# Another timetable in a fused attention and state-space kernel: projection two steps ahead, ScalarE's table blocks and GpSimd's products in chosen slots

## The chip, the cores and the metric

The kernel runs on one core of a Trainium2 chip. The metric is the device time of one launch in microseconds (us). A core has five engines with one instruction stream each, executed in order: TensorE (PE in the profile; its weight loads are PEld), VectorE (DVE), ScalarE (ACT), GpSimd (POOL) and SyncE (SP), which in this kernel issues nearly all DMA transfers. An engine waits at an instruction until the semaphores that this instruction names have been raised by others, and everything behind it in its stream waits too.

## The reference, cut to what matters

The input is a map of 2 x 256 x 256 positions with 128 channels, in float32. Layer 0 is a row-wise attention; it is not touched by the change. Layer 1 is a selective state-space layer over the 65,536 positions of each image, read as one sequence:

```python
xz = x @ in_proj_w.T                       # x: 128 channels, group-normalised; xz: 2 * 256
xi, z = jnp.split(xz, 2, axis=-1)
xi = silu(depthwise_conv_3x3(xi) + conv_b) # 256 channels
xs = xi.reshape(B, D_INNER, L)             # D_INNER = 256, L = 65536
x_dbl = jnp.einsum('bdl,cd->bcl', xs, x_proj_w[0])
dts, Bs, Cs = x_dbl[:, :8], x_dbl[:, 8:24], x_dbl[:, 24:]
delta = softplus(jnp.einsum('brl,dr->bdl', dts, dt_w[0]) + dt_b[0][None, :, None])
A = -jnp.exp(A_logs)                       # 256 x 16
# for each channel d and state n, along the sequence:
#   h = exp(delta * A) * h + (delta * xs) * B ;  y = sum over n of h * C
y = selective_scan(xs, delta, A, Bs, Cs, Ds)   # adds Ds * xs
y = layernorm(y) * ln_g + ln_b
y = y * silu(z)
return y @ out_proj_w.T                    # and the layer's input is added
```

## The kernel before, in words

First come statistics of layer 0, its attention and the statistics of layer 1; this stage ends at about 3,340 us and is the same in both kernels. The rest is the state-space layer. Each image is cut into 64 steps of four image rows, T = 1024 positions, so there are 128 steps. The 256 channels times 16 states of a step are computed in 32 **units** (NU = 32): a unit holds 32 channels times 4 states on the 128 partitions, and 1024 positions along the free dimension. A unit is named by h (half of the channels), m (four states) and q (32 channels).

The order of the work is written out by hand: a loop over **slots** t emits for each engine what belongs to slot t, and the streams of TensorE, VectorE, ScalarE and GpSimd keep that order. SP's stream is not fixed by hand; the framework orders it. In slot t stand, in this order: the loads for unit t+6 (`fetch`), GpSimd's product for unit t+2 (`drive`, hb = du * B), GpSimd's product of unit t-1 if that unit is "pooled" (`product`, yc = h * C), ScalarE's exponential of unit t+1 (`decay`, da = exp(delta * A), into one of two PSUM buffers), VectorE's `scan` of unit t and, if the unit is not pooled, its `product` on VectorE too, every fourth slot TensorE's sum over states (`add_up`), every sixteenth the copy of the sum to SBUF (`y_out`), then the pieces that were entered for this slot with `at(slot, piece)`, and last ScalarE's copy of the scan's last column (`remember`). A scan of a pooled unit writes over hb in SBUF, that of another over da in PSUM. Ten of 32 units are pooled: before, those with t * 10 % 32 < 10, that is 0, 4, 7, 10, 13, 16, 20, 23, 26, 29.

The pieces come from two functions. `project(k)` makes the inputs of step k's scans: `load` (raw rows), `begin`, `turn` and `normalise` (transposed and group-normalised xn), `keep` (two halo rows for the next step), `conv` (nine products on TensorE for each of four 512-wide groups; the three with one row offset dy are one piece), `conv_out`, `silu_xs`, `gate` and `gate_out` (z, one product for each group, and its copy into the tile sz), `silu_z`, `states` and `states_out` (delta's low-rank input, B and C), `size` and `size_out` (the argument of softplus, into the tile delta), `softplus`, and `times` (du = delta * xs, on GpSimd). xs, sz, B and C, delta and du are stored to DRAM and loaded again, spread over partitions, by `fetch` and by `finish`. `conv`, `gate`, `states`, `size` and `turn` share one PSUM buffer (tag "p"). The tiles xs, sz, delta and du have one buffer each. `finish(k)` normalises the rows of y, multiplies by silu(z), projects and writes the result; its ScalarE pieces stand in slots 6, 14, 22, 30 (`norm`), 0, 8, 16, 24 (`affine`) and 3, 11, 19, 27 (`leave`) of the step after, its row statistics on VectorE in slots 4, 12, 20, 28, its product with silu(z) on VectorE (`gated`) in slots 1, 9, 17, 25, and `scales` on GpSimd in 5, 13, 21, 29. `finish` is not changed.

Before, project(k) has base = 32 k - 36, so conv begins in slot 30 of step k-2 and the last piece stands in slot 25 of step k-1. silu_xs is in slot 14, the two softplus in 19 and 22, silu_z in 25. Exponential, silu and softplus need different tables in ScalarE, so each of these four blocks has a table load ahead of it and one ahead of the decay that follows.

Of the kernel before, what the change touches and what calls it, by code (L numbers as in the profile page):

```python
# [8 lines left out]
F32 = mybir.dt.float32  # L9
AF = mybir.ActivationFunctionType  # L10
ALU = mybir.AluOpType
# [4 lines left out]
P = 128  # L16
# [5 lines left out]
def attn_then_ssm_kernel(  # L22
# [26 lines left out]
    nc = tc.nc  # L49
# [5 lines left out]
    NH = DI // P  # L55
    NS = A_logs.shape[1]
    DR = dt_w.shape[2]
    TB = 512
# [72 lines left out]
    with tc.tile_pool(name="prep", bufs=1) as prep, tc.tile_pool(  # L131
        name="prep2", bufs=3
# [14 lines left out]
        for g in range(NCG):  # L147
            for m in range(NSG):
                nc.sync.dma_start(
                    out=alog_d[:, :, g, m],  # L150
                    in_=A_logs[g * CQ : (g + 1) * CQ, m * SR : (m + 1) * SR],
# [70 lines left out]
    with tc.tile_pool(name="st", bufs=2) as stp, tc.tile_pool(  # L222
        name="st_x", bufs=3
    ) as stx, tc.tile_pool(name="st_ps", bufs=2, space=PSUM) as st_ps:
        for b in range(B):
            stats = stp.tile([P, G, NT, 6], F32, name="stats")
            for k in range(NT):
                xt = stx.tile([P, TT, C], F32, name="xt")
                nc.sync.dma_start(
                    out=xt,  # L230
                    in_=x_tok[b, k * P * TT : (k + 1) * P * TT, :].rearrange(
                        "(p t) c -> p t c", p=P
                    ),
# [15 lines left out]
    with ExitStack() as actx:  # L249
# [117 lines left out]
        for b in range(B):  # L367
# [17 lines left out]
            for g in range(NG):  # L385
# [4 lines left out]
                for gr in range(G):  # L390
                    nc.vector.bn_stats(stats1[:, gr, g, :], x1g[:, :, :, gr * CG : (gr + 1) * CG])
                nc.gpsimd.dma_start(  # L392
                    out=x1[b][:, g * LG : (g + 1) * LG, :].rearrange("(i p) l c -> p i l c", p=P),
                    in_=x1g,
# [8 lines left out]
    T = R * W  # L403
    NSTEP = H // R
    NB = T // TB
    WP = W + 2
    RB = TB // W
    WT = W // P
    NU = NCG * NSG
    NM = NQ * NSG  # L410
    POOLED = 10
    s1 = ctx.enter_context(tc.tile_pool(name="s1", bufs=1))
    s2 = ctx.enter_context(tc.tile_pool(name="s2", bufs=2))
    s3 = ctx.enter_context(tc.tile_pool(name="s3", bufs=3))
# [6 lines left out]
    dr = ctx.enter_context(tc.tile_pool(name="dr", bufs=3, space=DRAM))  # L421
# [6 lines left out]
    def at(t, piece, *args):  # L428
        slots.setdefault(t, []).append((piece, args))
# [4 lines left out]
    def project(k):  # L434

        b, s = steps[k]
        rs, sh = gn1[b]
        base = k * NU - NU - 4
        n = min(R, H - 1 - R * s)
        v = given[k] = {}  # L440
        o = {}
# [127 lines left out]
            )  # L569

        def size_out(h, i):
            if i == 0:
                o["delta"] = s1.tile([P, T], F32, name="delta")
            nc.scalar.activation(
                o["delta"][:, i * TB : (i + 1) * TB],
                o["dt"],
                AF.Identity,
                bias=dtb_c[:, h : h + 1],
            )

        def softplus(h):
            nc.scalar.activation(o["delta"], o["delta"], AF.Softplus)
            if h == 0:
                v["delta"] = dr.tile([NH, P, T], F32, name="delta_d")
                v["du"] = dr.tile([NH, P, T], F32, name="du_d")
            nc.sync.dma_start(out=v["delta"][h], in_=o["delta"])

        def times(h):
            du = s1.tile([P, T], F32, name="du")
            nc.gpsimd.tensor_tensor(du, o["delta"], o["xs"][:, h, :], ALU.mult)  # L590
            nc.sync.dma_start(out=v["du"][h], in_=du)

        at(base - 12, load)
        at(base - 3, begin)
        for r in range(0, n, RB):
            at(base - 3 + r, turn, "raw", r, min(RB, n - r))
            at(base - 2 + r, normalise, 2 + r, min(RB, n - r))
        at(base - 1 + RB, keep)
        t = base + 2
        for h in range(NH):  # L600
            for i in range(NB):
                for dy in range(3):
                    at(t + dy, conv, h, i, dy)
                at(t + 3, conv_out, h, i)
                t += 4

        at(t, silu_xs)
        at(t, gate, 0, 0)
        at(t + 1, gate_out, 0, 0)
        at(t + 1, states, 0)  # L610
        at(t + 2, states_out, 0)
        at(t + 2, states, 1)
        at(t + 3, states_out, 1)
        at(t + 3, size, 0, 0)
        at(t + 4, size_out, 0, 0)
        at(t + 4, size, 0, 1)
        at(t + 5, size_out, 0, 1)
        at(t + 5, softplus, 0)
        at(t + 5, gate, 0, 1)
        at(t + 6, gate_out, 0, 1)  # L620
        at(t + 6, times, 0)
        at(t + 6, size, 1, 0)
        at(t + 7, size_out, 1, 0)
        at(t + 7, size, 1, 1)
        at(t + 8, size_out, 1, 1)
        at(t + 8, softplus, 1)
        at(t + 8, gate, 1, 0)
        at(t + 9, gate_out, 1, 0)
        at(t + 9, times, 1)
        at(t + 9, gate, 1, 1)  # L630
        at(t + 10, gate_out, 1, 1)
        at(t + 11, silu_z)

    def finish(k):

# [138 lines left out]
                )  # L774

    def pooled(t):
        return t % NU * POOLED % NU < POOLED

    def decay(t):
        k, h, m, q = unit(t)  # L780
# [12 lines left out]
    def scan(t):  # L793
        k, h, m, q = unit(t)
        u = units[t]
        st = states_of[steps[k][0]][:, h * NQ + q, m : m + 1]
        u["h"] = u["hb"] if pooled(t) else u["da"]
        nc.vector.tensor_tensor_scan(u["h"], u["da"], u["hb"], st, ALU.mult, ALU.add)  # L798
# [6 lines left out]
    def product(t):  # L805
        k, h, m, q = unit(t)
        u = units[t]
        u["yc"] = s8.tile([P, T], F32, name="yc")
        eng = nc.gpsimd if pooled(t) else nc.vector
        eng.tensor_tensor(u["yc"], u["h"], repeats["cc", k, h, m], ALU.mult)  # L810
# [34 lines left out]
    for k in range(len(steps)):  # L845
        project(k)
        finish(k)
# [8 lines left out]
    with tc.manual_schedule(engines=engines):  # L856
        for t in range(min(slots), max(slots) + 1):
            if 0 <= t + AHEAD < end:
                fetch(t + AHEAD)
            if 0 <= t < end and t % (NU * NSTEP) == 0:  # L860
                st = s1.tile([P, NCG, NSG], F32, name="state")
                nc.gpsimd.memset(st, 0.0)
                states_of[steps[t // NU][0]] = st
            if 0 <= t + 2 < end:
                drive(t + 2)
            if 0 <= t - 1 < end and pooled(t - 1):
                product(t - 1)
            if 0 <= t + 1 < end:
                decay(t + 1)
            if 0 <= t < end:  # L870
                scan(t)
                if not pooled(t):
                    product(t)
            if 0 <= t - 5 < end and (t - 5) % NQ == 0:
                add_up(t - 5)
            if 0 <= t - 6 < end and unit(t - 6)[2:] == (NSG - 1, 0):
                y_out(t - 6)
            for piece, args in slots.pop(t, ()):
                piece(*args)
            if 0 <= t < end:  # L880
                remember(t)
# [37 lines left out]
```

## Time and profile before

| what | value |
|---|---|
| median of 3 runs | 18,758.38 us (18,757.69 to 18,761.69) |
| the profiled execution | 18,753.55 us, its span 18,751.8 us |
| VectorE busy over the span | 15,569.1 us (83%) |
| GpSimd busy | 13,905.4 us (74%) |
| TensorE busy | 14,378.9 us (77%) |
| ScalarE busy | 11,203.5 us (60%) |
| DMA, mean over the span | 184 GB/s, SP's queue 52.6% of 16 engines |

The profile is of one execution. A group line names the source line, engine and operation, the tiles written and read, how many instructions it holds, then their busy time and the mean in ns of one, then the idle time of the engine just ahead of them and the engine and line that ended most of it. A timeline line begins with the start in us from the span's start and the time busy; a bracket at its end holds the idle time ahead and what ended it. Times of single instructions overlap a little, so sums of them can be some per cent above the time that passed. In the stretch from 3,500 to 18,700 us VectorE is busy 13,525.82 of 15,200 us and GpSimd 13,795.43.

### The profile page before, as it was taken

Reading aid. Unit: us, or ns where it says so; the run is one execution under the profiler, and the core shown is the slowest. Engines: PE = TensorE matmul, PEld = TensorE weight load, DVE = VectorE, ACT = ScalarE, POOL = GpSimd, SP = SyncE. Lnnn points to the kernel's source line nnn. Section 1 sums busy time; section 2 is a strip of 40 time slices with the busy share of each in tenths; the row PEclk is TensorE's granted clock in tenths of the full one; section 3 lists DMA queues with packets and bytes.
Section 4 is the critical chain, followed back from the end, with each engine's and each line's share of the span. In section 5 each row is a group of like instructions: output and inputs, shape, how many; then the busy total and the mean of one; then the engine's idle time right before and its main releaser. Section 6 shows DMA issues by size and latency. Waiting matters only on the chain. (4 is left out here: it accounts for less than half of the span.)

```text
span 18751.8 us, 175838 instructions
## 1 busy us (share of the span) xinstructions
PE 14378.9 (77%) x54327; PEld 6530.2 (35%) x54327; DVE 15569.1 (83%) x14782; ACT 11203.5 (60%) x18207; POOL 13905.4 (74%) x8236
## 2 busy tenths in 40 slices
PE   4999999777777777777777777777777777777776
PEld 3666666222222222222222222222222222222222
DVE  6555555688888888888888888888888888888888
ACT  2444444566666666666666666666666666666665
POOL 0000000699999999999999999999999999999998
PEclk7999999888888888888888888888888888888887
DMA  4111111566666666666666666666666656666664
GB/s 190 68 68 54 68 68 59 172 208 207 208 210 207 208 209 209 208 209 206 206 209 209 207 208 208 208 208 208 210 207 208 207 206 209 210 207 209 207 209 169
DMA packets 1428682, 3451.87 MB, mean 184 GB/s; under 512 B 121836, under 2 KB 712984, under 8 KB 1409304
## 3 DMA queue, kind: packets, MB, share of 16 engines
q1 hardware_dynamic: 1419032, 3373.50, 52.6%
q0 software_dynamic: 8704, 67.11, 0.8%
q8 instruction: 428, 7.01, 0.2%
q14 instruction: 518, 4.24, 0.1%
HBM read 2752.28 MB, written 687.88 MB: 183 GB/s over the span
## 5 line engine op out<-in xcount | busy, mean ns | idle before, releaser
L791 POOL TENSOR_TENSOR hb<-du_r,bb 128x1024 f32<-128x1024 f32 x4096 | 9556.8, 2357 | 0.2 <-issue 0.2
L798 DVE TENSOR_TENSOR_SCAN da<-da,state,hb 128x1024 f32<-128x1024 f32 x2816 | 6608.6, 2347 | 1360.3 <-ACT da L783 1203.4
L783 ACT ACTIVATE da<-delta_r,a_neg 128x1024 f32<-128x1024 f32 x4096 | 4574.6, 1117 | 484.5 <-DVE hb L798 408.3
L497 PE MATMUL u_ps<-xn,w_tap 128*128 128x512 f32 x9216 | 4444.8, 630 | 24.6 <-ACT xs L508 6.1
L810 DVE TENSOR_TENSOR yc<-da,cc 128x1024 f32<-128x1024 f32 x2816 | 3449.5, 1225 | 160.4 <-issue 1.8
L798 DVE TENSOR_TENSOR_SCAN hb<-da,state,hb 128x1024 f32<-128x1024 f32 x1280 | 2995.4, 2340 | 208.4 <-ACT da L783 122.0
L810 POOL TENSOR_TENSOR yc<-hb,cc 128x1024 f32<-128x1024 f32 x1280 | 3014.5, 2355 | 6.0 <-issue 4.6
L830 PE MATMUL y<-yc,sel 128*32 128x512 f32 x16384 | 2564.9, 665 | 146.9 <-POOL yc L810 141.2
L497 PEld LDWEIGHTS u_ps<-xn,w_tap 128*128 128x128 f32 x9216 | 1802.0, 205 | 2158.4 <-issue 1911.7
L803 ACT COPY state<-da 128x1 f32<-128x1 f32 x2816 | 437.0, 155 | 3142.3 <-DVE yc L810 3142.3
L392 POOL DMA_DIRECT2D x<-x1g x32 | 23.2, 726 | 3033.6 <-DVE x1g L360 3033.6
L545 PE MATMUL xd_ps<-xs,w_xp 128*64 128x512 f32 x1024 | 935.3, 1068 | 793.8 <-ACT state L803 705.7
L590 POOL TENSOR_TENSOR du<-delta,xs 128x1024 f32<-128x1024 f32 x256 | 599.1, 2340 | 899.2 <-ACT state L803 761.3
L830 PEld LDWEIGHTS y<-yc,sel 128*32 128x32 f32 x16384 | 525.7, 116 | 2047.9 <-issue 1270.0
L563 PE MATMUL dt_ps<-xd,w_dt 8*128 8x512 f32 x1024 | 696.1, 765 | 541.6 <-ACT sz L533 538.6
L522 PE MATMUL z_ps<-xn,w_z 128*128 128x512 f32 x1024 | 582.8, 651 | 612.7 <-ACT sz L533 483.4
L695 PE MATMUL yd<-ident,yn 128*128 128x128 f32 x2048 | 373.0, 312 | 813.8 <-ACT yn L683 813.8
L717 PE MATMUL o_ps<-xres,ident 128*128 128x256 f32 x1024 | 413.0, 491 | 520.6 <-DVE yg L713 520.5
L657 PE MATMUL yt<-ident,ys 128*128 128x128 f32 x2048 | 331.3, 285 | 529.7 <-ACT ob L730 529.7
L823 PE MATMUL y<-xr,d_diag 128*128 128x512 f32 x1024 | 722.4, 845 | 0.0
L720 PEld LDWEIGHTS o_ps<-w_out,yg 128*128 128x128 f32 x4096 | 671.0, 233 | 45.1
L312 ACT ACTIVATE e<-s_ps,nmx 128x256 f32<-128x256 f32 x1024 | 471.7, 472 | 355.4 <-DVE nmx L308 354.9
(134 smaller groups left out, 18302.7 us busy)
## 6 DMA issues: line engine op xcount, KB each, us to landing
bb<-bc_d SPq DMA_DIRECT2D x1024, 512.0 KB, 4.2
cc<-bc_d SPq DMA_DIRECT2D x1024, 512.0 KB, 4.9
delta_r<-delta_d SPq DMA_DIRECT2D x1024, 512.0 KB, 6.4
du_r<-du_d SPq DMA_DIRECT2D x1024, 512.0 KB, 4.8
xs_d<-xs SPq DMA_DIRECT2D x128, 1024.0 KB, 7.8
xr<-xs_d SPq DMA_DIRECT2D x256, 512.0 KB, 4.4
delta_d<-delta SPq DMA_DIRECT2D x256, 512.0 KB, 2.6
du_d<-du SPq DMA_DIRECT2D x256, 512.0 KB, 2.6
```

Source lines behind the costliest of these rows:

```text
L497: nc.tensor.matmul(o["u"], w_tap[:, h, 3 * dy + dx, :], o["xn"][:, i * RB + dy : i * RB + dy + RB, dx : dx + W], start=(dy == 0 and dx == ...
L522: nc.tensor.matmul(o["z"], w_z[:, h, :], o["xn"][:, 1 + i * RB : 1 + (i + 1) * RB, 1 : W + 1], start=True, stop=True,)
L545: nc.tensor.matmul(o["xd_ps"], w_xp[:, h, :], o["xs"][:, h, i * TB : (i + 1) * TB], start=(h == 0), stop=(h == NH - 1),)
L563: nc.tensor.matmul(o["dt"], w_dt[:, h, :], o["xd"][0:DR, i * TB : (i + 1) * TB], start=True, stop=True,)
L590: nc.gpsimd.tensor_tensor(du, o["delta"], o["xs"][:, h, :], ALU.mult)
L720: nc.tensor.matmul(o["o"][:, j, :], o["yg"][:, h, j * P : (j + 1) * P], w_out[:, h, :], start=False, stop=(j == WT - 1 and h == NH - 1),)
L783: nc.scalar.activation(da, spreads["delta", k, h, q], AF.Exp, scale=a_neg[:, g, m : m + 1])
L791: nc.gpsimd.tensor_tensor(hb, spreads["du", k, h, q], repeats["bb", k, h, m], ALU.mult)
L798: nc.vector.tensor_tensor_scan(u["h"], u["da"], u["hb"], st, ALU.mult, ALU.add)
L810: eng.tensor_tensor(u["yc"], u["h"], repeats["cc", k, h, m], ALU.mult)
L823: nc.tensor.matmul(y[:, cols], d_diag[:, h, :], xr[:, cols], start=True, stop=False)
L830: nc.tensor.matmul(y[q * CQ : (q + 1) * CQ, cols], sel, units[t + q]["yc"][:, cols], start=False, stop=(m == NSG - 1),)
```

## The change: what it does

The function `project` gets another timetable, and the set of pooled units is written out.

- base becomes 32 k - 64: every piece stands 28 slots earlier with respect to the scans of its step. conv begins in slot 2 of step k-2.
- gate and gate_out no longer follow the convolution; each stands behind the conv_out of its group.
- silu_xs stands in slot 20, one softplus over both halves in slot 28 (the tile delta holds both halves, and its store is one DMA), silu_z in slot 4 of the next step.
- times writes du over xs, in the slots 30 and 31, so the tile du is gone.
- pooled are 1, 7, 9, 12, 14, 16, 18, 23, 25, 31.

```diff
-    POOLED = 10
+
+    POOLED = (1, 7, 9, 12, 14, 16, 18, 23, 25, 31)
...
-        base = k * NU - NU - 4
+        base = k * NU - 2 * NU
...
-            if i == 0:
-                o["delta"] = s1.tile([P, T], F32, name="delta")
+            if (h, i) == (0, 0):
+                o["delta"] = s1.tile([P, NH, T], F32, name="delta")
             nc.scalar.activation(
-                o["delta"][:, i * TB : (i + 1) * TB],
+                o["delta"][:, h, i * TB : (i + 1) * TB],
...
-        def softplus(h):
+        def softplus():
             nc.scalar.activation(o["delta"], o["delta"], AF.Softplus)
+            v["delta"] = dr.tile([NH, P, T], F32, name="delta_d")
+            nc.sync.dma_start(out=v["delta"].rearrange("h p t -> p h t"), in_=o["delta"])
+
+        def times(h):
+
             if h == 0:
-                v["delta"] = dr.tile([NH, P, T], F32, name="delta_d")
                 v["du"] = dr.tile([NH, P, T], F32, name="du_d")
-            nc.sync.dma_start(out=v["delta"][h], in_=o["delta"])
-
-        def times(h):
-            du = s1.tile([P, T], F32, name="du")
-            nc.gpsimd.tensor_tensor(du, o["delta"], o["xs"][:, h, :], ALU.mult)
+            du = o["xs"][:, h, :]
+            nc.gpsimd.tensor_tensor(du, o["delta"][:, h, :], du, ALU.mult)
             nc.sync.dma_start(out=v["du"][h], in_=du)
 
-        at(base - 12, load)
-        at(base - 3, begin)
+        at(base - 14, load)
+        at(base - 5, begin)
         for r in range(0, n, RB):
-            at(base - 3 + r, turn, "raw", r, min(RB, n - r))
-            at(base - 2 + r, normalise, 2 + r, min(RB, n - r))
-        at(base - 1 + RB, keep)
+            at(base - 4 + r, turn, "raw", r, min(RB, n - r))
+            at(base - 3 + r, normalise, 2 + r, min(RB, n - r))
+        at(base, keep)
         t = base + 2
         for h in range(NH):
             for i in range(NB):
                 for dy in range(3):
                     at(t + dy, conv, h, i, dy)
                 at(t + 3, conv_out, h, i)
+                at(t + 3, gate, h, i)
+                at(t + 4, gate_out, h, i)
                 t += 4
-
+        t = base + 20
         at(t, silu_xs)
-        at(t, gate, 0, 0)
...
         at(t + 3, states_out, 1)
-        at(t + 3, size, 0, 0)
...
-        at(t + 11, silu_z)
+        t += 3
+        for h in range(NH):
+            for i in range(NB):
+                at(t, size, h, i)
+                at(t + 1, size_out, h, i)
+                t += 1
+        at(base + 28, softplus)
+        at(base + 30, times, 0)
+        at(base + 31, times, 1)
+        at(base + NU + 4, silu_z)
...
-        return t % NU * POOLED % NU < POOLED
+        return t % NU in POOLED
```

The numbers of GpSimd's, VectorE's and TensorE's instructions for a step stay as they are; ScalarE has one softplus of 128x2048 in place of two of 128x1024, and one pair of table loads less.

More of the change, by code (lines that the diff above doesn't have):

```diff
@@ L604, in project @@
                 at(t + 3, conv_out, h, i)
+                at(t + 3, gate, h, i)
+                at(t + 4, gate_out, h, i)
                 t += 4
+        t = base + 20
         at(t, silu_xs)
-        at(t, gate, 0, 0)
-        at(t + 1, gate_out, 0, 0)
         at(t + 1, states, 0)
@@ L613, in project @@
         at(t + 3, states_out, 1)
-        at(t + 3, size, 0, 0)
[L615 to L631, printed above, removed]
-        at(t + 11, silu_z)
+        t += 3
[8 more added lines that the diff above has]
+        at(base + NU + 4, silu_z)
     def finish(k):
```

## The prediction

> **What bounds the kernel now.** I read the page's engine rows and slices first, then the costliest groups, then the VectorE timeline of one step with the ScalarE, GpSimd and SP timelines beside it, then the end of the run. 15,270 of the 18,751.8 us are the scan stage (first scan at 3428.64, last product done at 18699.20), 128 steps of 32 slots. Two groups name what is lost there:
>
> ```profile
> L798 DVE TENSOR_TENSOR_SCAN da<-da,state,hb 128x1024 f32<-128x1024 f32 x2816 | 6608.6, 2347 | 1360.3 <-ACT da L783 1203.4
> L590 POOL TENSOR_TENSOR du<-delta,xs 128x1024 f32<-128x1024 f32 x256 | 599.1, 2340 | 899.2 <-ACT state L803 761.3
> ```
>
> VectorE stands idle 1,360 us ahead of its scans, nearly all of it for ScalarE's decay; GpSimd stands idle 899 us ahead of `du`, for ScalarE too. In the timeline the VectorE gap is this one:
>
> ```profile
> 10073.28 2.34 DVE L798 TENSOR_TENSOR_SCAN hb<-da,state,hb 128x1024 f32<-128x1024 f32 x1
> 10081.02 2.36 DVE L798 TENSOR_TENSOR_SCAN da<-da,state,hb 128x1024 f32<-128x1024 f32 x1 [5.39 <-ACT da L783]
> ```
> ```profile
> 10075.38 0.69 ACT L574 ACTIVATE delta<-dt_ps,dtb_c 128x512 f32<-128x512 f32 x1 [1.97 <-PE dt_ps L563]
> 10076.09 1.28 ACT L582 ACT_TABLE_LOAD   x1
> 10077.38 1.06 ACT L582 ACTIVATE delta<-delta 128x1024 f32<-128x1024 f32 x1
> ...
> 10078.50 1.28 ACT L783 ACT_TABLE_LOAD   x1
> 10079.80 1.12 ACT L783 ACTIVATE da<-delta_r,a_neg 128x1024 f32<-128x1024 f32 x1
> ```
>
> A softplus sits between two table loads, after a copy that waited for TensorE; the decay behind it comes at 10079.80, and the scan that needs it 5.39 us late. In this step the gaps ahead of scans are 0.95, 0.37, 2.42, 5.39 and twice 1.25: 11.6 us. The two 1.25 are another thing, shown here:
>
> ```profile
> 10024.34 2.34 DVE L798 TENSOR_TENSOR_SCAN hb<-da,state,hb 128x1024 f32<-128x1024 f32 x1
> 10026.71 1.12 ACT L783 ACTIVATE da<-delta_r,a_neg 128x1024 f32<-128x1024 f32 x1 [2.70 <-DVE hb L798]
> 10027.93 2.36 DVE L798 TENSOR_TENSOR_SCAN da<-da,state,hb 128x1024 f32<-128x1024 f32 x1 [1.25 <-ACT state L803]
> ```
>
> The decay starts only when the scan of a pooled slot has ended, and the next scan waits for it. In the built program's list of waits, ScalarE's decay takes that scan's end with it in slots 10, 20, 23 and 26 of each step.
>
> How long a step is, and how long without blocks:
>
> ```profile
> L516 ACT ACTIVATE xs<-xs x126: 1910/1910/1912, 3590.4 to 18524.0; 128x2048 f32<-128x2048 f32 x126
> ```
> ```profile
> 18591.98 2.34 DVE L798 TENSOR_TENSOR_SCAN hb<-da,state,hb 128x1024 f32<-128x1024 f32 x1
> ...
> 18697.97 1.23 DVE L810 TENSOR_TENSOR yc<-da,cc 128x1024 f32<-128x1024 f32 x1
> ```
>
> 125 periods in 14,933.6 us: **119.47 us a step**. The last step has no projection beside it; its 32 slots run from 18591.98 to 18699.20: **107.2 us**, VectorE without a gap. The difference, 12.3, is what there is to win.
>
> **The change part by part.** I write S4 for the start of scan 4 of a step. One unpooled slot is 3.52 us of VectorE (10106.36 to 10109.88), a pooled one 2.26, one with row statistics 4.67 (10095.93 to 10100.60).
>
> *Blocks.* Four (two silu of 1.91, two softplus of 1.06) become three of 128x2048; the joined softplus I take at 1.91, the silu's row for that shape. One pair of table loads goes. The three stand in slots 20, 28 and 4, each with row statistics, unpooled, the next slot unpooled too. In slot 20: decay to 1.25 after its start, load and silu to 4.45, VectorE's slot over at 4.67, state copy, load and decay to 7.2; the scan that needs it starts at 4.67 + 3.52 = 8.2. So the block fits with 1.0 to spare, and costs nothing. Its cover is the statistics and the unpooled slot; with a pooled slot in either place (1.26 less) it would come 0.3 late. Gain: all gaps of the blocks.
>
> This row is 1.28 a load, the next activation 1.29 after its start. The Trainium skill ("ScalarE: Activation LUTs", "What ACT_TABLE_LOAD costs") says that a drain of about 1.38 us belongs to each switch, 2.66 in all. By that the decay would end 9.8 into slot 20, 1.6 late at each of three blocks, and the sum below would be some 600 us higher (an estimate from that page); the rows show no such drain, so I go by them.
>
> *The decay tied to a pooled scan.* In the new program's list it stands in slots 7, 14 and 18: 3 x 1.25 = **3.75 a step**, that nothing hides. Below: 0 if GpSimd holds VectorE at those places anyway; above: 3.75.
>
> *Projection earlier.* Conv, x and z products, raw loads and stores are as many as before. SP's stores of xs, delta, du and sz are now needed a step later, so their landing costs nothing. The gate's product and copy are put between conv groups, which share one PSUM buffer: from the end of the gate's copy (2.85 into slot 6: decay 1.25, row normalising 1.0, copy 0.6) to the next conv copy (1.25 into slot 9, so 11.8 after slot 6 begins) are 8.95 us. Nine conv products take 7.99 (3364.33 to 3372.32), transposes between them 0.65. They fit by 0.3, so they cost nothing; a late one holds ScalarE at the copy, and the decay behind it, for slot 11, has 2.8 to spare. Its cover gone, each further us is one on the step.
>
> *One sz tile.* silu of z now ends at S4 + 4.45, and the next step's first gate copy, in slot 6, writes the same tile: it waits for the store. Its place without a wait is S4 + 10.4; the decay behind it is held by scan 7 until S4 + 14.05 anyway. In the trace:
>
> ```profile
> 10087.35 1.91 ACT L538 ACTIVATE sz<-sz 128x2048 f32<-128x2048 f32 x1
> ```
> ```profile
> 10090.77 2.81 SPq L769 DMA_DIRECT2D du_r<-du_d  x2
> 10093.68 0.55 SPq L645 DMA_DIRECT2D xres<-x  x1
> 10094.31 0.42 SPq L540 DMA_DIRECT2D sz_d<-sz  x1
> ```
> ```profile
> DMA to landing us min/median/max: 4.8/6.2/8.4
> ```
>
> The store waits 5 us in SP's queue and lands 6.2 later: 11.2 after the silu. In the new order it stands behind bb, which waits for GpSimd's drive of slot 7. Unblocked it lands at 4.45 + 0.4 + 6.2 = 11.0: no cost. As in the trace, 15.65, copy and state copy to 16.4: decay and scan 8 are 2.35 late. I take the middle, **1.2**, because SP's wait for a drive is the commoner case but only in part 5 us long. The Trainium skill ("Trainium Kernel Development and Optimization", "Best Practices") asks for two buffers where transfer and compute overlap; with no overlap at all, the copy would wait the row's 6.2 in full, 780 us in 126 steps, against 150 by the slack counted here.
>
> *GpSimd.* 32 drives at 2.32 (6.96 for three), 10 products at 2.33, two du at 2.32, four groups of row scales at 1.54 (10036.31 to 10037.85), 1.2 for halo copies: 74.2 + 23.3 + 4.6 + 6.2 + 1.2 = **109.5**. It is under VectorE's 107.2 + 3.75, so it does not bound, but by 1.5 only. Six of ten products lie in slots 7 to 18: there GpSimd needs 38.7 us and VectorE, with its waits, 37.3. The drives are two slots ahead, which covers 1.4. The du products now follow softplus by two slots and wait no more. Cost 0 to 1.1 (the drive for slot 3, behind du, halo and the products of 31 and 1); I take 0.
>
> *Start and end.* A second projection lies ahead of the first scan. From rows of the first: conv 4 x 8.77, gates 4 x 2.4, silu 3.2, x products 5.2, size 9.6, softplus 3.2, transposes 3.9: **+70**, less 2 for the softplus joined in the first. Bounds: 38 (conv alone) and 76 (the whole first chain, 3347.5 to 3423.3). The last two steps run without blocks: 2 x 107.2.
>
> *Sum.* Step 107.2 + 3.75 + 1.2 = 112.15. Span: 3428.6 + 68 + 126 x 112.15 + 214.4 + 52.6 (from the last product to the end) = 17,894.5. The profiled run took 1.8 more than its span and the median of three is 4.8 above that: **17,901**.
>
> **The rivals.**
> *GpSimd and SP set the pace.* VectorE faster means GpSimd at 98%; each lag delays bb, so sz, so the gate copy, then TensorE's conv. For it: 109.5 against 111; the trace's SP rows wait up to 11.9 for a drive. Against: slots 19 to 30 hold two products in which GpSimd catches up. With 2.35 for sz, 1.1 for the drive and half a slot, 1.2, for a conv that is late: 115.6 a step, 18,336.
> *The blocks are still late.* If the joined block does not fit and loses 1.5 in each of three places on top of the forecast: 116.65, 18,468. For it: only 1.0 to spare, and row normalising in slots 6, 22 and 30 waits for GpSimd's scales. Against: the last step's rows show those copies without a gap.
> *Slower.* The sz store alone: every step it is late enough that scan 8 waits. Break-even is (18,751.8 - 3,496.6 - 267) / 126 = 118.95 a step, 8 over 110.95, so landing at S4 + 21.3, 16.8 after the silu. SP's longest wait (11.9) with the longest landing (8.4) is 20.3, which would give 11.5 a step: 19,200. Against: that needs the worst of both always; 11.2 is what the trace shows.
>
> **How the numbers follow.** Forecast 0.64 (its own range 17,720 to 18,130: sz 0 and a start of 38, up to sz 2.35 and 0.6 for the drive); pace of GpSimd and SP 0.20; blocks late 0.08; slower 0.06; no change 0.02 (within 0.2%, about what a measurement here can tell). Range 17,650, where part of the 3.75 is hidden, to 18,330, which leaves the late blocks, the slower case and a little of the pace case out. Faster 0.92, same 0.02, slower 0.06.
>
> **What would show it.** A silu period near 112; idle of L798 for decay down from 1,203 to some 600, in gaps of 1.25 after the pooled scans of 7, 14 and 18; no wait of du for ScalarE; three blocks a step with no gap behind them; the first gate copy of a step waiting for the store of sz, 1 us or more; GpSimd near 97%; first scan near 3,497. Wrong if scans wait for hb from GpSimd more than 1 us a step, if the gate copy holds scan 8 by over 2.4, or if conv copies wait for TensorE by over 2 us.

## The result, and the profile after

The changed kernel took 18,762.4 us (median of 4 runs, 18,745.6 to 18,768.9) against 18,758.0 of the kernel before beside it (18,752.6 to 18,761.7): ratio 1.0001, interval 0.9984 to 1.0019. No change, where 17,901 and a range of 17,650 to 18,330 were predicted. The profiled execution took 18,764.65 us, its span 18,762.9; the first scan starts at 3502.85 us, 74.2 later than before.

The length of a step stands in the row of the silu of xs (count, min/median/max in ns, first and last start), here from 3,600 us on:

```profile
L517 ACT ACTIVATE xs<-xs x125: 1910/1912/1916, 3691.0 to 18452.9; 128x2048 f32<-128x2048 f32 x125
```

124 periods in 14,761.9 us are **119.05 us a step**, where 112.15 were predicted and 119.47 measured before. 126 x 0.42 = 53 us are won in the steps, and the start, 74.2 later, more than takes them back.

The groups of the page that answer to those shown of before, and a third:

```profile
L791 DVE TENSOR_TENSOR_SCAN da<-da,state,hb 128x1024 f32<-128x1024 f32 x2816 | 6607.8, 2347 | 1567.2 <-ACT state L796 857.7
...
L534 ACT COPY sz<-z_ps 128x512 f32<-128x512 f32 x512 | 299.2, 584 | 1246.1 <-DMA sz_d<-sz 1095.1
...
L592 POOL TENSOR_TENSOR xs<-delta,xs 128x1024 f32<-128x1024 f32 x256 | 601.4, 2349 | 47.5 <-ACT delta L583 47.2
```

`du`'s wait for ScalarE is gone (899 to 47 us), but VectorE's idle time ahead of its scans has risen, from 1,360 to 1,567 us, and its cause has another name: not ScalarE's decay that is late, but ScalarE's state copy, 857.7 us. The second row says what ScalarE did then: the gate copy waits 1,095.1 us for the store of sz, 126 times, 8.7 us each.

In slot 20 (and in slot 4) the block does what the prediction said. ScalarE and VectorE in slot 20 of a step (start, duration, engine and line):

```profile
10112.18 1.12 ACT L776 ACTIVATE da<-delta_r,a_neg 128x1024 f32<-128x1024 f32 x1
10113.32 1.28 ACT L517 ACT_TABLE_LOAD   x1
10114.61 1.91 ACT L517 ACTIVATE xs<-xs 128x2048 f32<-128x2048 f32 x1
...
10116.59 1.28 ACT L776 ACT_TABLE_LOAD   x1
10117.88 1.12 ACT L776 ACTIVATE da<-delta_r,a_neg 128x1024 f32<-128x1024 f32 x1
```
```profile
10111.87 2.35 DVE L791 TENSOR_TENSOR_SCAN da<-da,state,hb 128x1024 f32<-128x1024 f32 x1
...
10120.06 2.35 DVE L791 TENSOR_TENSOR_SCAN da<-da,state,hb 128x1024 f32<-128x1024 f32 x1
```

Scan 20 starts at 10111.87; the decay behind the silu ends 7.13 later (7.2 predicted), and the scan that needs it starts 8.19 later (8.2), with no gap ahead of it.

The block in slot 28, the softplus, does not always fit. Here are ScalarE's rows of one step and VectorE's scan 30 behind them; scan 28 of this step began at 10019.20:

```profile
10021.02 0.69 ACT L575 ACTIVATE delta<-dt_ps,dtb_c 128x512 f32<-128x512 f32 x1 [1.63 <-PE dt_ps L564]
...
10022.92 1.28 ACT L583 ACT_TABLE_LOAD   x1
```
```profile
10028.71 2.36 DVE L791 TENSOR_TENSOR_SCAN da<-da,state,hb 128x1024 f32<-128x1024 f32 x1 [1.25 <-ACT da L776]
```

The last copy of `size_out` waited for TensorE, so the block's table load begins 3.72 after scan 28, not 1.45 as in slot 20, and scan 30 is 1.25 late. Of 124 steps of the changed kernel 21 have such a gap, 0.25 us a step on average. This sits beside the main loss; in the experiments it grows.

What the step loses most by, in the timelines of ScalarE, TensorE, SP and VectorE one after the other; scan 4 of this step began at 10047.95:

```profile
10050.69 1.91 ACT L539 ACTIVATE sz<-sz 128x2048 f32<-128x2048 f32 x1
...
10067.36 0.59 ACT L534 COPY sz<-z_ps 128x512 f32<-128x512 f32 x1 [8.86 <-DMA sz_d<-sz]
```
```profile
10068.00 5.31 PE L498 MATMUL u_ps<-xn,w_tap 128*128 128x512 f32 x6 [10.90 <-ACT state L796]
```
```profile
10053.96 0.52 SPq L755 DMA_DIRECT2D bb<-bc_d  x1
...
10055.83 0.59 SPq L762 DMA_DIRECT2D du_r<-du_d  x1
10056.52 0.54 SPq L541 DMA_DIRECT2D sz_d<-sz  x1
```
```profile
10069.13 2.36 DVE L791 TENSOR_TENSOR_SCAN da<-da,state,hb 128x1024 f32<-128x1024 f32 x1 [7.13 <-ACT state L796]
10076.22 2.36 DVE L791 TENSOR_TENSOR_SCAN da<-da,state,hb 128x1024 f32<-128x1024 f32 x1 [0.58 <-issue]
10080.82 2.36 DVE L791 TENSOR_TENSOR_SCAN da<-da,state,hb 128x1024 f32<-128x1024 f32 x1 [0.99 <-ACT da L776]
10094.79 2.36 DVE L791 TENSOR_TENSOR_SCAN da<-da,state,hb 128x1024 f32<-128x1024 f32 x1 [1.26 <-ACT da L776]
10108.34 2.36 DVE L791 TENSOR_TENSOR_SCAN da<-da,state,hb 128x1024 f32<-128x1024 f32 x1 [1.25 <-ACT da L776]
```

The silu is done at 10052.60. SP issues the store 3.9 us later: bb, ahead of it, stood until GpSimd's drive ended at 10053.93, and four loads of 512 KB (bb, cc, delta_r, du_r) go out ahead of it. The store, 1 MB, then needs 10.8 us to land. Over 124 steps of the trace the store is issued 2.9 to 5.8 us after the silu, 5.2 in the median; it lands 19.4 after scan 4 began, in the median of the 97 landings on record among them, the same as here. The gate copy waits 8.86 us, and scan 8 behind it 7.13; 0.58 and 0.99 follow, because TensorE's next convolution waited 10.90 us for the PSUM buffer that the copy held, and the copy of its result, at 10078.93, still waited 2.80 for TensorE. The last two rows are the tied decays after the pooled slots 14 and 18. All gaps here sum to 11.2: 107.2 + 11.2 is 118.4, of the 118.75 that this step took.

The store's issue-to-landing time in the whole run, and the DMA engines while it was under way (window, busy time of PE, PEld, DVE, ACT and POOL, granted clock, DMA busy share, GB/s):

```profile
DMA to landing us min/median/max: 5.3/9.5/11.0
```
```profile
10060.00:10067.30 7.30, 0.00 (x0) 0.00 (x0) 2.00 (x1) 0.00 (x0) 7.13 (x4) 0.50 0.99 349
```

The median was 6.2 in the profile before; here it is 9.5. The 16 DMA engines are 99% busy in that stretch, while TensorE and ScalarE do nothing at all.

### The profile page after: what moved, and what is told of

It reads as the page before. It is cut to its first block, busy times and chain, and to the rows that moved or that the text cites. A ratio compares the mean times of both kernels' runs of the same rounds, so it can differ in the third digit from the quotient of the medians.

```text
span 18762.9 us, 174718 instructions
## 1 busy us (share of the span) xinstructions
PE 14208.9 (76%) x54327; PEld 6542.0 (35%) x54327; DVE 15563.3 (83%) x14782; ACT 10829.8 (58%) x17822; POOL 13925.4 (74%) x8236
## 5 line engine op out<-in xcount | busy, mean ns | idle before, releaser
L791 DVE TENSOR_TENSOR_SCAN da<-da,state,hb 128x1024 f32<-128x1024 f32 x2816 | 6607.8, 2347 | 1567.2 <-ACT state L796 857.7
L498 PE MATMUL u_ps<-xn,w_tap 128*128 128x512 f32 x9216 | 4629.0, 652 | 1353.7 <-ACT state L796 1099.8
L823 PE MATMUL y<-yc,sel 128*32 128x512 f32 x16384 | 2687.8, 712 | 823.1 <-POOL yc L803 820.6
L546 PE MATMUL xd_ps<-xs,w_xp 128*64 128x512 f32 x1024 | 703.4, 825 | 702.8 <-ACT xd L559 558.1
L509 ACT ACTIVATE xs<-u_ps,cb_c 128x512 f32<-128x512 f32 x512 | 351.7, 687 | 1225.8 <-PE u_ps L498 1210.1
L534 ACT COPY sz<-z_ps 128x512 f32<-128x512 f32 x512 | 299.2, 584 | 1246.1 <-DMA sz_d<-sz 1095.1
L696 ACT ACTIVATE yd<-yd,lnb_c,lng_c 128x256 f32<-128x256 f32 x1024 | 544.5, 532 | 635.5 <-PE yd L688 618.3
L476 PE MATMUL t_ps<-ident,raw 128*128 128x128 f32 x1020 | 231.8, 368 | 705.3 <-ACT xn L481 588.3
L688 PE MATMUL yd<-ident,yn 128*128 128x128 f32 x2048 | 472.9, 375 | 264.0 <-ACT yn L676 264.0
L592 POOL TENSOR_TENSOR xs<-delta,xs 128x1024 f32<-128x1024 f32 x256 | 601.4, 2349 | 47.5 <-ACT delta L583 47.2
L713 PEld LDWEIGHTS o_ps<-w_out,yg 128*128 128x128 f32 x4096 | 618.0, 216 | 42.2
```

Of the source, the lines that this page charges most:

```text
L498: nc.tensor.matmul(o["u"], w_tap[:, h, 3 * dy + dx, :], o["xn"][:, i * RB + dy : i * RB + dy + RB, dx : dx + W], start=(dy == 0 and dx == ...
L546: nc.tensor.matmul(o["xd_ps"], w_xp[:, h, :], o["xs"][:, h, i * TB : (i + 1) * TB], start=(h == 0), stop=(h == NH - 1),)
L592: nc.gpsimd.tensor_tensor(du, o["delta"][:, h, :], du, ALU.mult)
L688: nc.tensor.transpose(o["yd"][:, h, j * P : (j + 1) * P], o["yn"][:, j, h * P : (h + 1) * P], ident,)
L696: nc.scalar.activation(o["yd"][:, h, :], o["yd"][:, h, :], AF.Identity, bias=lnb_c[:, h : h + 1], scale=lng_c[:, h : h + 1],)
L713: nc.tensor.matmul(o["o"][:, j, :], o["yg"][:, h, j * P : (j + 1) * P], w_out[:, h, :], start=False, stop=(j == WT - 1 and h == NH - 1),)
```

## The experiments

Ratios are to the kernel before, run beside each. A step length is taken from the row of the silu of xs as above. Source lines of the changed kernel are meant where nothing else is said.

### Taking the wait for the store away (e1)

The silu of z writes into the tile delta, which is idle until size_out in slot 24, and the store reads that tile. The gate copies then wait for the silu alone.

```diff
-            nc.scalar.activation(o["sz"], o["sz"], AF.Silu)
+            nc.scalar.activation(o["delta"], o["sz"], AF.Silu)
...
-            nc.sync.dma_start(out=v["sz"].rearrange("h p t -> p h t"), in_=o["sz"])
+            nc.sync.dma_start(out=v["sz"].rearrange("h p t -> p h t"), in_=o["delta"])
```

> The changed kernel with one edit: silu of z reads sz and writes into the tile of delta, which stands idle from slot 0 to slot 24, and the store of sz is taken from there. So the next step's first gate copy no longer waits for that store. Theory A (the store of sz is what ate the gain: the copy waited 8.7 us a step for it): the step falls from 119.05 to about 110.2, which is 107.2 of VectorE, two decays tied to a pooled scan (slots 14 and 18 in this build) at 1.25 each, and 0.5 for the rest; first scan still near 3,503; in all 17,660. Rival B (GpSimd, SP or TensorE set the pace, and the copy's wait is only where it shows): the wait moves to another place, the step stays above 116, 18,390 or more.

Measured: 17,733.5 us, ratio 0.9454 (0.9440 to 0.9468); 110.82 us a step. The groups of its page:

```profile
L791 DVE TENSOR_TENSOR_SCAN da<-da,state,hb 128x1024 f32<-128x1024 f32 x2816 | 6603.3, 2345 | 588.4 <-ACT da L776 426.4
...
L534 ACT COPY sz<-z_ps 128x512 f32<-128x512 f32 x512 | 298.8, 584 | 229.7 <-PE z_ps L523 229.5
```

No copy waits for the DMA any more, and the scans' idle time falls from 1,567 to 588 us. What is left to the decay is 426.4 / 126 = 3.4 us a step. By the trace this is two things: the ties of slots 14 and 18, 1.25 each in every step, and the softplus in slot 28, behind which scan 30 is late in 54 of 124 steps, 0.69 a step on average. No gap stands ahead of scan 8: its decay begins 1.3 to 2.0 us before pooled scan 7 ends, so in this build slot 7 has no tie. The store still takes 9.6 us to land (median), and nobody waits for it. So with the one wait 119.05 - 110.82 = **8.2 us a step** went, 1,029 us in all; up to 1.25 of it would have been the tie of slot 7, had the wait not covered it.

### Issuing the store at once, from ScalarE (e2)

```diff
-            nc.sync.dma_start(out=v["sz"].rearrange("h p t -> p h t"), in_=o["sz"])
+            nc.scalar.dma_start(out=v["sz"].rearrange("h p t -> p h t"), in_=o["sz"])
```

> The changed kernel with one edit: the store of sz is issued by ScalarE itself, right behind its silu, instead of by SP, where it stood 4 us behind a load that waits for GpSimd. sz still has one buffer. Theory A1 (the place in SP's queue is about half of the wait, the landing the other half): the store goes out 4 us earlier, and, no longer behind four loads of 512 KB, lands in 6.2 to 7 instead of 9.5; the copy waits 2 us or less, the step is 111 to 113, 17,770 to 18,020. Rival A2 (the landing is slow because of all transfers in flight, wherever it is issued): it waits 4 to 5 us still, step 114 to 115, 18,200.

Measured: 17,728.1 us, ratio 0.9451 (0.9437 to 0.9465). The store's timeline row in ScalarE's queue, the first load of SP behind it, and the store's landing:

```profile
10054.27 0.37 ACTq L541 DMA_DIRECT2D sz_d<-sz  x1
```
```profile
10054.90 0.52 SPq L755 DMA_DIRECT2D bb<-bc_d  x1
```
```profile
DMA to landing us min/median/max: 3.9/4.0/9.5
```

Same tile, same wait, same transfer: issued 0.6 us ahead of the four loads instead of 0.7 behind them it lands in 4.0 us, not 9.5, and the copy waits once in the whole run. Here too scan 8 has no gap.

### The same queue, but behind the loads (e11)

e2 changed two things, the queue and the place in the order of transfers. Here ScalarE issues the store, but in slot 6.

```diff
-            nc.sync.dma_start(out=v["sz"].rearrange("h p t -> p h t"), in_=o["sz"])
+
+        def store_z():
+            v["sz"] = dr.tile([NH, P, T], F32, name="sz_d")
+            nc.scalar.dma_start(out=v["sz"].rearrange("h p t -> p h t"), in_=o["sz"])
...
+        at(base + NU + 6, store_z)
```

> The changed kernel with the sz store issued by ScalarE, so outside SP's queue, but two slots after the silu: ahead of the row normalising of slot 6, some 1 us later than SP issued it, when the four loads of the next unit are already under way. It separates the two halves of the store's delay. Theory L (the transfer waits behind loads that are under way, whatever queue it is issued from: DMA share 0.99 between issue and landing): it lands 9 to 11 us after its issue, the gate copy waits 8 to 9.5 us, and the time is 18,700-18,900 us. Theory Q (what cost it was SP's in-order queue; on a queue of its own it lands as in the run where ScalarE issued it at once, in 4.0 us): landing about 13.7 us after scan 4 begins, the copy waits 2 to 3.5, the step loses 0.4 or so, 17,730-17,850 us.

Measured: 18,730.6 us, ratio 0.9987 (0.9978 to 0.9997), 118.71 us a step. The store stands in ScalarE's queue behind four loads and the raw rows in SP's:

```profile
10043.48 0.60 SPq L447 DMA_DIRECT2D raw<-x  x1
10044.16 0.40 ACTq L543 DMA_DIRECT2D sz_d<-sz  x1
...
10053.75 0.58 ACT L534 COPY sz<-z_ps 128x512 f32<-128x512 f32 x1 [7.54 <-DMA sz_d<-sz]
```

It lands in 6.0/10.0/10.8 us (min, median, max), and the copy waits 1,056.4 us in 127 times. Theory L holds: the landing goes by the loads that are under way ahead of the store, not by the queue that issues it. The other part of the delay, the time from the silu to the issue, is about as long here (4.4 us in the median, by the slot chosen) as in SP's queue (5.2); issuing at once, as in e2, takes both away.

### The gates one convolution group later (e9)

```diff
-                at(t + 3, gate, h, i)
-                at(t + 4, gate_out, h, i)
+                if (h, i) != (0, 0):
+                    at(t + 3, gate, (h * NB + i - 1) // NB, (i - 1) % NB)
+                    at(t + 4, gate_out, (h * NB + i - 1) // NB, (i - 1) % NB)
                 t += 4
+        at(base + 18, gate, NH - 1, NB - 1)
+        at(base + 19, gate_out, NH - 1, NB - 1)
```

> The changed kernel with each gate piece one convolution group later: the first gate copy of a step stands in slot 10 instead of 6; the sz tile, its store and SP's queue are as they are. Theory S (the copy waits for the store of sz, which lands about 19.4 us after scan 4 begins): without a wait the copy's place in slot 10 is 20.4 + 1.25 = 21.7 after scan 4 begins, later than the landing, so the wait falls from 8.7 us to under 0.5 and the time to that of the runs without it, 17,720-17,800 us. Rival C (the gate products between the convolution groups, on one PSUM buffer, are themselves what holds ScalarE and TensorE): the products and copies are as many and as close as before, the step stays near 119 and the time over 18,500.

Measured: 17,752.4 us, ratio 0.9464 (0.9450 to 0.9479), 111.0 us a step. The copy's group:

```profile
L534 ACT COPY sz<-z_ps 128x512 f32<-128x512 f32 x512 | 298.6, 583 | 78.0 <-PE z_ps L523 74.7
```

The store lands as late as in the changed kernel (median 9.6), but the copy comes later still. One tile was enough, with the first gate copy four slots later. Rival C, the gate products between the convolution groups as the cause, falls: they are as many and as close as before.

### The set of pooled units (e3, e4)

e3 is the kernel before with the new set alone; e4 is e1 with the old set.

```diff
-    POOLED = 10
+    POOLED = (1, 7, 9, 12, 14, 16, 18, 23, 25, 31)
...
-        return t % NU * POOLED % NU < POOLED
+        return t % NU in POOLED
```

> The kernel before with the new set of pooled units alone, the old timetable kept. Theory: the set has no worth of its own; two tied decays fewer (slots 14 and 23 instead of four) give back 2.5 a step at most, and blocks now stand in slot 14 and beside 23 and 25, which are pooled and shorter, losing about as much: 18,500 to 19,000. Rival: the spacing of GpSimd's products was part of what held the kernel back: below 18,400.

Measured: 18,768.6 us, ratio 1.0004 (0.9994 to 1.0013): no change.

```diff
-    POOLED = (1, 7, 9, 12, 14, 16, 18, 23, 25, 31)
+    POOLED = (0, 4, 7, 10, 13, 16, 20, 23, 26, 29)
```

> As the first of these runs (silu of z written into the tile of delta), with the old set of pooled units: 0, 4, 7, 10, 13, 16, 20, 23, 26, 29. Then two of three blocks begin in a pooled slot (4 and 20) and the third (28) has one behind it. By the slot sums each block is then 0.3 late, 1 us a step in all, and the tied decays are again two: 17,790. If keeping products away from the blocks is what carries the change, it loses 2 us or more at each block: 18,400. If the set does not matter, it stands within 40 us of the first run.

Measured: 17,837.5 us, ratio 0.9508 (0.9494 to 0.9523). The new set is worth 104 us, 0.86 a step, beside the new timetable, and nothing alone. In this kernel the old set puts pooled units into slots 4 and 20, where the blocks are, and the trace shows the scans behind them late: scans 6 and 22, each by 0.34 us in nearly every step. That is the 0.3 that the prediction gave for a pooled slot there. The ties are again two, ahead of scans 11 and 30.

### The tied decays (e8, e10, e5)

In the built programs, each tied decay has been given the same PSUM buffer as the unit just before it. (Why the pool of two buffers hands it out so, perhaps because it expects a pooled unit's buffer to be free early, no run here shows.) Two tags with one buffer each force strict alternation.

```diff
-    ps_d = ctx.enter_context(tc.tile_pool(name="ps_d", bufs=2, space=PSUM))
+    ps_d = ctx.enter_context(tc.tile_pool(name="ps_d", bufs=1, space=PSUM))
...
-        da = units[t]["da"] = ps_d.tile([P, T], F32, name="da")
+        da = units[t]["da"] = ps_d.tile([P, T], F32, name="da", tag=f"da{t % 2}")
```

In the kernel before:

> The kernel before with the decays' two PSUM buffers in strict alternation and nothing else changed. If the tied decays cost what the prediction read in the profile before (two clean gaps of 1.25 a step, in slots 10 and 26, and two hidden in the gaps of the blocks): 126 x 2.5 = 315 less, 18,445 us; if all four count, 126 x 5 = 630 less, 18,130. If GpSimd's waits for ScalarE and the blocks hold the step at 119.5 whatever VectorE gains: 18,700-18,760.

Measured: 18,330.2 us, ratio 0.9771 (0.9756 to 0.9785); 116.05 us a step, 3.4 less than before. That lies between the two cases, and the trace shows where: 1.25 is gone ahead of scan 11, 1.45 ahead of scan 21, 0.57 ahead of scan 27 and 0.35 ahead of scan 19, while scan 24 behind a softplus waits 0.41 more. This edit of two lines does for the kernel before what the whole change did not.

In the changed kernel:

> The changed kernel with the decays' two PSUM buffers in strict alternation and nothing else changed: the wait for the store of sz stays, the ties go. If the two costs add (ties of 1.25 after pooled slots 7, 14 and 18 beside the sz wait; the one of slot 7 is merged with it): 2 x 1.25 to 3.4 a step less, 18,765 - 126 x 2.5 to 3.4 = 18,340-18,450 us. If what VectorE gains after slot 14 only makes the next sz wait longer, since the store's issue waits for GpSimd and SP: within 50 us of 18,765.

Measured: 18,406.7 us, ratio 0.9813 (0.9796 to 0.9829); 116.16 us a step, 2.9 less, within the first theory's 2.5 to 3.4. The composition is another: the two ties are gone (2.5) and the wait for the store is shorter (1.9 less ahead of scans 8, 10 and 11; the store is issued 3.2 after the silu in the median, not 5.2), but scan 30 behind the softplus is now late in 111 of 124 steps, 1.5 a step more. So the costs do not simply add; the sum fits in part by luck. The gate copy still waits, 913 us in 126 times.

With the store's wait gone (e1 and the tags):

> The sz-free kernel of the first experiment (17,733.5 us, a step of 109.7), with the decays' two PSUM buffers given in strict alternation, so that no decay shares the buffer of the unit just before it; nothing else is changed. Theory T (VectorE with its ties sets the step: 107.2 + 2 x 1.25 = 109.7): the 1.25 after the pooled slots 14 and 18 go, the step falls to 107.2-108 and the time to 17,420-17,520 us. Theory G (GpSimd sets the step: it is busy 13,412 of 13,700 us there, 97.9%, with no wait ahead of its drives): the ties go from VectorE's rows, scans wait for GpSimd's hb instead, the step stays at 109.5-109.8 and the time at 17,700-17,740.

Measured: 17,598.5 us, ratio 0.9380 (0.9366 to 0.9394), which neither number had. The step is 109.73, theory G's number; but it was taken from a step of 109.7 in e1, which was one step: e1's mean, by its silu row, is 110.82. The windows of e5 and e1 from 3,600 to 17,300 us (columns as in the window above):

```profile
3600.00:17300.00 13700.00, 10795.45 (x38944) 4288.38 (x38943) 13226.58 (x9239) 9143.74 (x13859) 13538.69 (x7989) 0.85 0.67 226
```
```profile
3600.00:17300.00 13700.00, 10703.73 (x38550) 4291.50 (x38551) 13093.35 (x9147) 9044.93 (x13717) 13412.37 (x7911) 0.84 0.66 224
```

Without ties (first row) GpSimd is busy 13,538.69 of 13,700 us, 98.8%, or 108.4 us a step. Of the 2.5 that the two ties cost, 1.1 comes back. What takes the rest is mixed, as the scans' group in this window says:

```profile
L791 DVE TENSOR_TENSOR_SCAN da<-da,state,hb 128x1024 f32<-128x1024 f32 x2747 | 6440.4, 2345 | 280.8 <-ACT da L776 129.1 <-issue 76.5 <-POOL hb L784 66.8
```

GpSimd's product ends 66.8 of the 280.8 us, ScalarE's decay 129.1. GpSimd has 1.3 us a step left and is near its limit; that it alone sets this step is not shown.

### Nine pooled units (e6, e7)

```diff
-    POOLED = (1, 7, 9, 12, 14, 16, 18, 23, 25, 31)
+    POOLED = (1, 7, 9, 12, 16, 18, 23, 25, 31)
```

On top of e2; first without, then with the alternating buffers.

> The kernel with the sz store on ScalarE's queue (17,728.1 us), with nine pooled units instead of ten: unit 14's product goes from GpSimd to VectorE. GpSimd's step falls by 2.36 to 107.3, VectorE's work without ties rises by 1.26 to 108.5. Theory G (GpSimd set the step at 109.7): 108.5 plus what ties remain, up to 2.5, so 17,580-17,890 us, and below 17,700 only if at most one tie remains. Theory T (VectorE with its ties set it): at least 109.7 + 1.26 less the tie that goes with unit 14, so no faster than 17,720.

Measured: 17,695.8 us, ratio 0.9432 (0.9417 to 0.9446), 110.41 us a step. One tie is left, 1.25 ahead of scan 19. The time lies inside theory G's range and 24 us below theory T's bound, so it does not decide between them.

> As the run with nine pooled units, and the decays' two PSUM buffers in strict alternation, so no ties. Theory G: VectorE's 108.5 is the longest of the engines' steps, so 17,728 - 126 x 1.2 = 17,577 us (17,540-17,620). Theory T with no limit from GpSimd: 108.5 too, the same time; the two differ in the run without ties and with ten pooled units. If it stays at or above 17,700, a limit that neither names (TensorE's convolution chain, loads) holds the step at 109.7.

Measured: **17,544.0 us**, ratio 0.9350 (0.9335 to 0.9366), 109.23 us a step: the fastest version of the study. VectorE's work is 107.2 + 1.26 = 108.46, and its scans' group names what is left:

```profile
L791 DVE TENSOR_TENSOR_SCAN da<-da,state,hb 128x1024 f32<-128x1024 f32 x2944 | 6901.7, 2344 | 256.8 <-POOL state L855 160.8
```

160.8 of the 256.8 us is the wait ahead of the first scan; the other 96 are 0.76 a step, 0.57 of it ahead of scan 30, behind the softplus, in 43 of 124 steps. VectorE sets the step, with little else in its way.

## Why the prediction was wrong

The step that failed is *One sz tile*. It saw the wait and its mechanism, and sized it at 1.2 us a step between 0 and 2.35. It measured 8.2 (changed kernel against e1), or 7 if the tie of slot 7, which the prediction counted apart, is taken out. Three parts of it:

- *The queue* was priced right in its worse case: 5 us there, 5.2 measured in the median, 3.9 in the step shown. Taking a middle between this case and no wait was not: the store waited at least 2.9 in every step.
- *The landing* was not. The 6.2 was the median of a row whose store followed other transfers. The new slot 4 puts it behind four loads that go out together when one GpSimd drive has ended, so 9.5 in the median and 10.8 in the step shown. e2 and e11 show that this is a matter of the loads ahead: 4.0 us ahead of them, 10.0 behind them, both in ScalarE's queue. The prediction even named bb as standing ahead of the store, and left the landing at its old value.
- *What follows.* Landing at 19.4 after scan 4 gives, by the prediction's own arithmetic (copy and state copy, then the decay at 20.15 instead of 14.05), 6.1 us. The trace has 0.58 + 0.99 more behind it, since TensorE's convolution waits for the PSUM buffer that the copy holds. 107.2 + 3.75 + 6.1 + 1.6 = 118.6 (the tie of slot 7 is inside the 7.13 of scan 8 here); 119.05 was measured.

The slower rival was therefore the right mechanism, and its break-even, landing 21.3 after scan 4, was near: the knock-on brought it down to about 19.4. It was thought unlikely because it "needs the worst of both always". It did not need that: the queue's wait was the common 5 us, not 11.9, and the landing, 9.5 in the median, lay above the longest of the old row (8.4). In a timetable that repeats each step, such a wait comes always: 126 times.

Where the idle time ahead of the scans stands, in us a step, averaged over 124 steps of each trace (gaps above 0.15 us):

| ahead of scan | changed kernel | e1 | e2 | e10 | e5 | e7 |
|---|---|---|---|---|---|---|
| 8, 10, 11: the store's wait and what follows | 8.40 | 0 | 0 | 6.54 | 0.06 | 0 |
| 15, 19: decays tied to slots 14 and 18 | 2.52 | 2.65 | 2.63 | 0 | 0.62 | 0.12 |
| 30: behind the softplus in slot 28 | 0.25 | 0.69 | 0.69 | 1.72 | 0.83 | 0.57 |
| all | 11.20 | 3.39 | 3.38 | 8.40 | 2.28 | 0.73 |

What e5 and e7 have in the second row is no tie: other waits stand ahead of scan 19 there.

The Trainium skill ("Trainium Kernel Development and Optimization", "Best Practices") asks for two buffers where transfer and compute overlap. This case agrees, at a higher price than the 6.2 us that the prediction gave it: the copy waited 8.7 us a step on the one tile, and e1, where the silu writes another tile, lost that wait. But e9 shows that one buffer serves as well, if what writes it next comes four slots later.

The other steps:

- *Blocks*: right in slots 4 and 20, where margins came out as computed, to 0.1 us. Wrong in slot 28: the sum there left out the copies of `size_out`. In the steps with a gap the last one waits for TensorE, and the block begins 3.9 us after scan 28 in the median instead of 1.45. The cost was 0.25 a step, and 0.69 with the store's wait gone (e1), where 0 was put. What makes TensorE late in some steps and not in others was not followed.
- *Tied decays*: 2.5 for 3.75. Each tie cost the 1.25 predicted, in slots 14 and 18. That of slot 7 shows in no run: the store's wait covers it in the changed kernel, and in e1, e2 and e9 it is not there.
- *Projection between conv groups, cost 0*: no cost to the scans where the copy is not held, but not because the products fit by 0.3. In e1 the copy of the convolution still waits for TensorE, 876.9 us in 390 times (2.2 each), and ScalarE's slack covers it.
- *GpSimd*: no limit at 110.8 a step, as said (109.5 predicted, 13,412.37 / 13,700 x 110.82 = 108.5 measured). It comes near its limit at 109.7 (e5, 98.8% busy). The sums of 38.7 and 37.3 for "slots 7 to 18" come out with eleven drives and five products, slots 7 to 17. The rival in which GpSimd and SP set the pace did not happen.
- *Start*: +74.2 for +68, inside its bounds of 38 and 76.
- *Sum*: without the term of the store, 17,901 - 126 x 1.2 = 17,750. The kernels that do away with that wait took 17,733.5 and 17,728.1. That this is so near is partly luck: the ties cost 1.25 a step less than predicted, and the softplus and smaller gaps about as much more (110.95 predicted without the store, 110.82 in e1).

So where the expected gain went: the late blocks cost about 9 us a step before (119.47, less 107.2, less the 3.4 of e8's ties). All but 0.25 of that was removed, as planned, and some 8 came back as one wait of ScalarE for one store. The start took the rest.

## What to carry to other kernels

Here a transfer's landing time belonged to its place in the order of transfers, not to the transfer: 4.0 us or 10.0. When an edit moves a store, list what is issued in the few microseconds ahead of it, on every queue, and price the landing with that. Where one tile is written, stored and written again, write down the slot of the silu, of the issue, of the landing and of the next write, and take each from the new place, not from a row of the old one, since a fixed timetable meets it in every step. Count every piece that stands ahead of a block in its slot, with what that piece waits for: the copies of `size_out` were left out of the sum for slot 28. When a profile shows a short, regular wait of one engine for another's buffer, look at which buffer the pool gave: alternation by hand was worth 2.3% in the kernel before.

## What the runs showed of the hardware

- The 1 MB store of sz landed in 4.0 us (median) when issued 0.6 us ahead of four 512 KB loads, and in 9.5 to 10.0 behind them; the queue it was issued from, SP's or ScalarE's, made no such difference (9.5 and 10.0). In the stretch of the changed kernel shown above, the DMA engines were 99% busy at 349 GB/s meanwhile.
- A silu's table load of 1.28 us began 0.02 after the decay ended, and its activation 1.29 after the load's start; the next load began 0.07 after the activation ended (slot 20). No further time for the switch appears in these rows.
- With the products as they are, GpSimd kept 98.8% busy over 13,700 us (e5) beside VectorE at 13,226.58 / 13,700 = 96.5%, and one 128x1024 product on it still took 2.36 us, as in the kernel before.
